# Two fused transformer layers on one core: one input sequence loaded in 32x32 squares and transposed by VectorE, and a set of TensorE transposes moved behind the last quantized down tile

## Chip, cores and metric

One core of a Trainium2 chip runs the whole program. The metric is the device time of that core in microseconds, the median of several runs. Times inside the profile count from the start of its span.

## What is computed

Two layers are applied to x of 2 sequences by 512 rows by 512 features, each layer an attention and a feed-forward part, each part followed by a residual sum and a layer norm:

```
x = layernorm(x + L0_attn(x))     x = layernorm(x + L0_ffn(x))
x = layernorm(x + L1_attn(x))     x = layernorm(x + L1_ffn(x))

L0_attn:  q   = elu(x @ Wq.T + bq) + 1             # only head 0 of each group of 4 is used: 8 heads of 128
          num = q @ M[h] ;  den = q @ z[h] + 1e-6
          out = repeat(num / den, 4) @ Wo.T        # so the four Wo blocks of a group can be summed first
L0_ffn:   ternary weights; silu(gate) * up and the down product are each scaled, clipped and truncated to int8
L1_attn:  q, k, v = x @ Wqkv + b ;  softmax(q k / sqrt(128)) v @ Wo + bo      # one head of 128
L1_ffn:   (silu(x @ Wg.T) * (x @ Wu.T)) @ Wd.T
```

The memory M and z of the first attention are only read; their update is not part of the result.

## The kernel before

The kernel is one long program in Tile. Engines work their own instruction queues strictly in order. A scheduler arranges the instructions of TensorE, VectorE, ScalarE and SyncE from the order of the program text and its own estimates when the kernel is built; GpSimd keeps the order of the text (`manual_schedule`, L59). `tc.issue_after` ties an instruction to stand behind another one. SyncE issues nearly all DMAs. They use eight completion semaphores in turn, so a DMA waits on its queue until the eighth DMA before it has landed, and whatever stands behind it waits too.

**First attention, set-up (L284 to L469).** Rows of x arrive in tiles of 128 rows (`load_x`, L74). A product needs x with the features on the partitions, so each sequence is turned: `transposed` (L106) makes 16 TensorE transposes of 128x128 (L115) into PSUM and copies them (L119), odd k on VectorE and even k on ScalarE, into a tile `xt` of 128 x 4 x 512. `queries` (L328) makes one head of one sequence: four matmuls over k (L334), exp and relu on ScalarE (L340, L342), and their combination on VectorE (L344). Sequence 0 comes first, heads 0 to 7, then sequence 1.

Between the queries the weights are prepared. Each head's Wo arrives as two tiles of 128x1024 (L306), from the pool `wop`, which has six buffers, thus three heads' worth (`pair_tile`, L276). `sum_weights` (L355) adds the two tiles (L358), which frees one of them, and adds the halves of the result (L360), which frees the other. GpSimd does this for heads 0, 3, 5 and 7, VectorE for 1, 2, 4 and 6. `fold` (L363) multiplies M[h] with the summed Wo (matmul pmw, L365) and ScalarE writes the result into `mw` (L368); GpSimd has put z into the last column of mw before (L326). With mw, `read` (L370) needs one matmul per head and row tile (L379).

SyncE's queue in this part holds, in order: two row tiles of x, the eight query weights with bq and z, the four row tiles of sequence 1, m, the Wo tiles of heads 0 to 5, the first gate-and-up tile of the quantized feed-forward part (gu0_0, L242, placed at h == 6, L302), the Wo tiles of heads 6 and 7, the other ten gate-and-up tiles, and small weights.

The scale of the ternary gate-and-up weights is the largest value of gu0_0: `largest` (L182, VectorE) takes it per partition, `over_partitions` (L189) turns it on TensorE (pmx_up), and `scales` (L200) spreads it (pbc_up). These two small TensorE instructions stand among the queries of sequence 1, behind query 1 and query 2. After that each gate-and-up tile is divided by the scale on ScalarE and compared on VectorE (`check_up`, L417).

**End of the quantized feed-forward part (L608 to L679).** There are eight down tiles, one for each sequence and 128 rows. For tile i, `down` (L590) makes the matmuls pd, `scaled` (L610) writes the scaled result (ScalarE) and cuts it (VectorE), `added` (L616) truncates on ScalarE (`truncated_parts`, L168), adds the row tile of x on VectorE (L621, L622) and takes the norm's statistics, and `layernorm_apply` (L152) normalises. `f0_down(i)` (L625) runs these steps staggered: down and scaled of tile i, added of i-1, the norm of i-2. The 16 transposes of sequence 0 for the second attention (`xt_a1`, L677) stand in the text before the last down tile; in the built program the first four of them come before its matmuls and twelve behind. The products of q and k (pqk, L778) follow.

```
        for i in range(2, len(order) - 1):
            f0_down(i)
        xt_a1 = [transposed(xs[0], "a10")]
        for i in range(len(order) - 1, len(order) + 2):
            f0_down(i)
```

Of the kernel before, what the change touches and what calls it, by code (L numbers as in the profile page):

```python
# [10 lines left out]
F32 = mybir.dt.float32  # L11
# [3 lines left out]
AF = mybir.ActivationFunctionType  # L15
ALU = mybir.AluOpType
# [3 lines left out]
P = 128  # L20
B, S, HID = 2, 512, 512
NT = S // P
NK = HID // P
NH, G, D = 8, 4, 128
# [3 lines left out]
LN_EPS = 1e-5  # L28
DEN_EPS = 1e-6
LAST = HID - 1  # L30
LENT = 3
TOP12 = -4096
BELOW_HALF = 0.5 - 2.0**-13
# [3 lines left out]
def kernel(  # L37
# [19 lines left out]
    nc = tc.nc  # L57
# [14 lines left out]
    xs = [[], []]  # L72

    def load_x(b):  # L74
        for t in range(NT):
            x = xp.tile([P, HID], F32, tag="x", name=f"x_{b}_{t}")
            eng = nc.scalar if b == 0 and t % 2 else nc.sync
            eng.dma_start(x, x_in[b, ts(t, P), :])
            xs[b].append(x)
# [2 lines left out]
    bq = const.tile([D, NH], F32, tag="bq", name="bq")  # L82
    z = const.tile([D, NH], F32, tag="z", name="z")

    ident = const.tile([P, P], F32, tag="ident", name="ident")
    make_identity(nc, ident)
    ln_eps = const.tile([P, 1], F32, tag="ln_eps", name="ln_eps")
# [4 lines left out]
    nc.vector.memset(den_eps, DEN_EPS)  # L92
    below_half = const.tile([P, 1], F32, tag="below_half", name="below_half")
    nc.vector.memset(below_half, -BELOW_HALF)
    ones = const.tile([P, P], F32, tag="ones", name="ones")
    nc.vector.memset(ones, 1.0)


    rise = psum("rise")
# [4 lines left out]
    copies = []  # L104
# [47 lines left out]
    def layernorm_apply(out, row, stats):  # L152
        mv, rstd = stats
        nc.vector.tensor_scalar(
            out, row, mv[:, 0:1], rstd, ALU.subtract, ALU.mult
        )
# [5 lines left out]
    def truncated_parts(pool, y, n, name):  # L162

        a = pool.tile([P, S], I8, tag="tr_a", name=f"ta_{name}")  # L168
        b = pool.tile([P, S], I16, tag="tr_b", name=f"tb_{name}")
        nc.scalar.activation(a[:n], y, AF.Relu, bias=below_half[:n])  # L170
        nc.scalar.activation(b[:n], y, AF.Relu, bias=below_half[:n], scale=-1.0)  # L171
        return a, b
# [111 lines left out]
    with tc.tile_pool(name="a0w", bufs=1) as a0w, tc.tile_pool(name="a0", bufs=2) as a0:  # L284
        wq = []
        for h in range(NH):
# [5 lines left out]
            if h == 0:  # L292
                nc.sync.dma_start(bq, bq_in)
                nc.sync.dma_start(z, z_in)
        load_x(1)
        m = a0w.tile([D, NH, D], F32, tag="m", name="m")
        nc.sync.dma_start(m, m_in)

        wos = []
        for h in range(NH):  # L300
            halves = []
            if h == 6:  # L302
                gus = up_weights(gu0_in, "0", range(1))
            for j in range(2):
                w = pair_tile(f"wo{h}_{j}")
                nc.sync.dma_start(w, wo0_in[h, :, ts(j, G // 2), :])  # L306
                halves.append(w)
            wos.append(halves)

        gus += up_weights(gu0_in, "0", range(1, len(CHUNKS)))  # L310
        wqkv = const.tile([P, NK, 3 * D], F32, tag="wqkv", name="wqkv")
# [10 lines left out]

        mw = a0w.tile([D, NH, HID], F32, tag="mw", name="mw")
        nc.gpsimd.tensor_copy(mw[:, :, LAST], z)  # L326

        def queries(b, xt, h, cuts=1):  # L328

# [33 lines left out]
        def fold(h):  # L363
            p = psum(f"pmw_{h}")
            nc.tensor.matmul(p, m[:, h, :], wos[h], start=True, stop=True)  # L365
            c = small.tile([P, 1], F32, tag="col", name=f"col_{h}")
            nc.scalar.mul(c, p[:, LAST:], -1.0)
            nc.scalar.activation(mw[:, h, :LAST], p[:, :LAST], AF.Identity, bias=c)  # L368

        def read(b, t, between):  # L370

            x = xs[b][t]
            ys, steps = [], []
            for h0 in range(0, NH, 4):
                four = []
                den = small.tile([P, 4], F32, tag="den", name=f"den_{b}_{t}_{h0}")
                for j in range(4):
                    po = psum(f"po0_{b}_{t}_{h0 + j}")
                    nc.tensor.matmul(  # L379
                        po, qs[b][h0 + j][:, ts(t, P)], mw[:, h0 + j, :],  # L380
                        start=True, stop=True,
                    )
                    nc.scalar.activation(
                        den[:, j : j + 1], po[:, LAST:], AF.Identity, bias=den_eps
                    )
                    four.append(po)
                nc.vector.reciprocal(den, den)
                for j in range(4):
                    d = den[:, j : j + 1]
                    if h0 + j < LENT:  # L390
                        y = a0.tile([P, HID], F32, tag="y", name=f"y_{b}_{t}_{j}", bufs=3)
                        nc.scalar.activation(  # L392
                            y[:, :LAST], four[j][:, :LAST], AF.Copy, scale=d
                        )
                        if ys:
                            nc.gpsimd.tensor_add(  # L396
                                ys[0][:, :LAST], ys[0][:, :LAST], y[:, :LAST]
                            )
                        ys.append(y)
                    else:  # L400
                        steps.append(nc.vector.scalar_tensor_tensor(  # L401
                            x[:, :LAST], four[j][:, :LAST], d, x[:, :LAST], ALU.mult, ALU.add
                        ))
            between(steps)
            nc.gpsimd.tensor_add(x[:, :LAST], x[:, :LAST], ys[0][:, :LAST])
            return steps
# [25 lines left out]
        for h in range(NH):  # L432
            queries(0, xt, h, 1 if h else 2)
            if h == 4:
                sum_weights(nc.gpsimd, 0)
                turn_memory()
                sum_weights(nc.vector, 1)
            elif h == 6:
                xt1 = transposed(xs[1], "a01")
                sum_weights(nc.vector, 2)  # L440
        sum_weights(nc.gpsimd, 3)
        for h in range(NH):
# [81 lines left out]
    with tc.tile_pool(name="f0", bufs=2) as f0:  # L524
# [85 lines left out]
        def scaled(i):  # L610
            y = f0.tile([P, HID], F32, tag="y", name=f"yd_{i}")
            moved[i] = nc.scalar.activation(y, pds[i], AF.Copy, scale=down_scale)
            cut_to_12(y)
            ys[i] = y

        def added(i):  # L616
            b, t = order[i]
            ta, tb = truncated_parts(f0, ys[i], P, f"d{i}")

            x = xs[b][t]  # L620
            nc.vector.scalar_tensor_tensor(x, tb, 128.0, x, ALU.min, ALU.subtract)  # L621
            nc.vector.scalar_tensor_tensor(x, x, -1.0, ta, ALU.mult, ALU.add)  # L622
            stats[i] = layernorm_stats(x, f"f0_{i}")

        def f0_down(i):  # L625
            if i < len(order):
                pds[i] = down(*order[i])
                scaled(i)
            if 0 <= i - 1 < len(order):
                added(i - 1)  # L630
            if 0 <= i - 2 < len(order):

                b, t = order[i - 2]
                with tc.issue_after(taken[f"f0_{min(i, len(order)) - 1}"].ins):
                    layernorm_apply(xs[b][t], xs[b][t], stats[i - 2])

        to_divide[2:2] = [None, None]
        for c in range(3):
# [35 lines left out]
        up(1, 10, moved.values())  # L674
        for i in range(2, len(order) - 1):
            f0_down(i)
        xt_a1 = [transposed(xs[0], "a10")]  # L677
        for i in range(len(order) - 1, len(order) + 2):
            f0_down(i)  # L679

    gus = up_weights(gu1_in, "1", range(6, len(CHUNKS)))
# [487 lines left out]
```

## Time and profile before

| | |
|---|---|
| median of three runs | 481.75 us (481.19, 481.75, 482.28) |
| the profiled execution | 481.89 us |
| its span, from the first to the last instruction | 479.7 us |
| TensorE (PE) busy | 470.9 us, 98% of the span |
| VectorE (DVE) busy | 349.9 us, 73% |
| ScalarE (ACT) busy | 272.5 us, 57% |
| GpSimd (POOL) busy | 115.1 us, 24% |
| TensorE transposes (L115) that the change touches | 16 of sequence 1 from 32.14 us; 16 of sequence 0 from 233.47 us (4) and 236.47 us (12) |
| load of a 512 KB gate-and-up tile | 7.9 us to landing (median of 20) |

How to read it: the page divides the span into 40 slices and gives each engine's busy share of each slice in tenths. A group line names the program line, engine and operation, then the result and its operands, the shapes, how often, the busy time, the mean of one in ns, and the idle time just before with what ended it. A timeline line begins with its start in us and its duration; several alike in a row are merged, with their number behind an x. In the list of waits the columns are who waited, for whom, and then us in total, how many times, and the longest. PEld is TensorE's loading of the stationary operand, SPq is SyncE's queue. A row of a table by windows gives the window, its length, each engine's busy time with its instructions, and then the granted TensorE clock, the busy share of the DMA engines and GB/s. A float32 matmul appears as two records.

### The profile page before, as it was taken

The page shows a single profiled execution, that of the slowest core. Times are in us where ns is not written, and L with a number is a line of the kernel's source. Part 1 is how long each engine was busy: PE and PEld are TensorE (multiplying, and loading weights), DVE is VectorE, ACT ScalarE, POOL GpSimd, SP SyncE. Part 2 cuts the span into 40 slices and gives each one's busy share as a digit, 9 for nine tenths or more (in the row PEclk, how much of TensorE's full clock was granted, in tenths as well). Part 3 has the DMA queues.
Part 4 walks back from the last instruction along what each step waited for, and adds up shares of the span by engine and source line. Part 5 has one row for each costly group of instructions (what it writes and reads, how often), then busy time and mean ns, then how long its engine had stood idle before and what let it go on. Part 6 is the DMA issues. An engine that isn't in the chain of part 4 may idle for free.

```text
span 479.7 us, 5815 instructions
## 1 busy us (share of the span) xinstructions
PE 470.9 (98%) x1891; PEld 329.6 (69%) x1891; DVE 349.9 (73%) x689; ACT 272.5 (57%) x512; POOL 115.1 (24%) x146
## 2 busy tenths in 40 slices
PE   9999999999999999999999999999999999999995
PEld 8454444434487788787766567888788888888885
DVE  1345677677666586756979989997875778999852
ACT  3344899556666867546645834686753565434221
POOL 0344102666530392000464032000000000023211
PEclk9999999999999999999999999999999999999998
DMA  8999700000043001121390000000000000001011
GB/s 303 389 357 336 296 2 0 0 0 1 2 128 110 3 1 26 65 91 34 113 385 2 0 1 1 1 1 0 1 0 1 1 1 1 0 23 40 27 45 44
DMA packets 13748, 33.98 MB, mean 71 GB/s; under 512 B 1872, under 2 KB 2768, under 8 KB 13712
## 3 DMA queue, kind: packets, MB, share of 16 engines
q1 hardware_dynamic: 13280, 32.85, 19.0%
q10 hardware_dynamic: 432, 0.66, 0.4%
q8 instruction: 22, 0.36, 0.3%
q14 instruction: 14, 0.11, 0.1%
HBM read 31.40 MB, written 2.10 MB: 70 GB/s over the span
## 4 chain that ended last, share of the span: by engine, by line
PE 71%; ACT 7%; DVE 5%; issue 3%; POOL 1%; POOLq 0%; DVEq 0%; ACTq 0%
PE pm L977 17%; PE pg_f L539 9%; PE pc L977 9%; PE pu_f L539 9%; PE pdm L1052 7%; PE pd_f L595 4%; PE pdc L1052 4%; DVE x L401 4%; PE pqk L778 3%; PE po L379 2%; ACT y L392 2%; ACT t L411 2%; PE pv L791 1%; PE po L880 1%; PE pot L863 1%
## 5 line engine op out<-in xcount | busy, mean ns | idle before, releaser
L379 PE MATMUL po<-mw,q 128*128 128x512 f32 x128 | 57.1, 598 | 0.4 <-DVE mv_a L142 0.2
L334 PE MATMUL pq<-xt_a,wq 128*128 128x512 f32 (+1 forms) x136 | 56.4, 567 | 0.0
L148 POOL TENSOR_TENSOR rstd_f<-mv_f,ln_eps 128x1 f32<-128x1 f32 x15 | 4.7, 313 | 185.8 <-DVE mv_f L1063 132.1
L379 PEld LDWEIGHTS po<-mw,q 128*128 128x128 f32 x128 | 23.0, 189 | 32.2 <-issue 17.7
L334 PEld LDWEIGHTS pq<-xt_a,wq 128*128 128x128 f32 x136 | 25.5, 190 | 27.5 <-issue 25.5
L977 PE MATMUL pm<-r,it_early 128*128 128x512 f32 x144 | 37.8, 393 | 0.4 <-ACT r L718 0.4
L977 PE MATMUL pm<-r,ugu 128*128 128x512 f32 (+1 forms) x144 | 36.8, 393 | 0.0
L977 PEld LDWEIGHTS pm<-r,it_early 128*128 128x128 f32 x144 | 27.0, 188 | 6.7 <-ACT r L718 0.7
L401 DVE SCALAR_TENSOR_TENSOR x<-po,den,x 128x511 f32<-128x511 f32 x40 | 29.8, 745 | 1.9
L977 PEld LDWEIGHTS pm<-r,ugu 128*128 128x128 f32 (+1 forms) x144 | 26.8, 186 | 6.3
L170 ACT ACTIVATE ta_f<-y_f,below_half 128x512 int8<-128x512 f32 (+1 forms) x22 | 15.9, 722 | 24.4 <-DVE y_f L160 23.9
L988 DVE SCALAR_TENSOR_TENSOR ev_q<-pm,ev_q 128x512 f32<-128x512 f32 (+1 forms) x28 | 19.2, 687 | 14.0 <-PE pm L977 14.0
L396 POOL TENSOR_TENSOR y<-y,y 128x511 f32<-128x511 f32 x16 | 20.3, 1270 | 31.5 <-ACT y L392 30.8
L565 DVE SCALAR_TENSOR_TENSOR it_f<-tb_f,ta_f 128x512 fp32r<-128x512 int16 (+1 forms) x22 | 15.2, 690 | 16.0 <-ACT tb_f L171 15.9
L977 PE MATMUL pc<-r,ugu 128*128 128x512 f32 (+1 forms) x96 | 26.1, 394 | 0.0
L340 ACT ACTIVATE e<-pq,bq 128x512 f32<-128x512 f32 x16 | 11.1, 693 | 25.8 <-PE pq L334 25.8
L413 POOL TENSOR_SCALAR td<-wd,inv_down 128x512 fp32r<-128x512 f32 (+1 forms) x11 | 19.5, 1792 | 24.8 <-DVE inv_down L204 24.4
L539 PE MATMUL pg_f<-xh,tu 128*128 128x512 f32 (+1 forms) x88 | 25.1, 405 | 0.0
L539 PE MATMUL pu_f<-xh,tu 128*128 128x512 f32 (+1 forms) x88 | 24.0, 394 | 0.0
L539 PE MATMUL pg_f<-xl,tu 128*128 128x512 f32 (+1 forms) x88 | 23.9, 393 | 0.0
L539 PE MATMUL pu_f<-xl,tu 128*128 128x512 f32 (+1 forms) x88 | 23.9, 393 | 0.0
L987 ACT ACTIVATE ev_q<-pc 128x512 f32<-128x512 f32 (+1 forms) x28 | 16.4, 591 | 12.1 <-PE pc L977 12.1
(292 smaller groups left out, 1106.0 us busy)
## 6 DMA issues: line engine op xcount, KB each, us to landing
gu<-in_gu SPq DMA_DIRECT2D x20, 512.0 KB, 7.9
wo<-in_wo SPq DMA_DIRECT2D x16, 512.0 KB, 7.6
wd<-in_wd SPq DMA_DIRECT2D x20, 256.0 KB, 4.7
wq<-in_wq SPq DMA_DIRECT2D x8, 256.0 KB, 4.5
out<-x SPq DMA_DIRECT2D x7, 256.0 KB, 2.0
x<-in_x SPq DMA_DIRECT2D x6, 256.0 KB, 5.4
gu<-in_gu SPq DMA_DIRECT2D x2, 384.0 KB, 6.5
wqkv<-in_wqkv SPq DMA_DIRECT2D x1, 768.0 KB, 10.8
```

What stands on the lines that cost most here:

```text
L170: nc.scalar.activation(a[:n], y, AF.Relu, bias=below_half[:n])
L334: nc.tensor.matmul(pq[:, at], wq[h][:, k, :], xt[:, k, at], start=(k == 0), stop=(k == NK - 1),)
L379: nc.tensor.matmul(po, qs[b][h0 + j][:, ts(t, P)], mw[:, h0 + j, :], start=True, stop=True,)
L396: nc.gpsimd.tensor_add(ys[0][:, :LAST], ys[0][:, :LAST], y[:, :LAST])
L401: steps.append(nc.vector.scalar_tensor_tensor(x[:, :LAST], four[j][:, :LAST], d, x[:, :LAST], ALU.mult, ALU.add))
L413: eng.tensor_scalar(out, w, factor, None, ALU.mult)
L539: nc.tensor.matmul(pp[a][:n], t[:, a, i % NK, :n], x2[b][i], start=(i == 0), stop=(i == 2 * NK - 1),)
L595: nc.tensor.matmul(pd, inter[b][c][:n, ts(t, P)], td[c][:n].bitcast(F32R), start=(c == 0), stop=(c == last),)
L977: nc.tensor.matmul(p[:n], w, x, start=(left[id(p)] == begun[id(p)]), stop=(left[id(p)] == 1))
L987: nc.scalar.activation(ev[:n], pc, AF.Copy, scale=CROSS)
L988: nc.vector.scalar_tensor_tensor(ev[:n], pm, MAIN, ev[:n], ALU.mult, ALU.add)
L1052: nc.tensor.matmul(p[:, :w], got[j // 4][1][kind][:n, j % 4], down_parts[j][kind][:, cols], start=(j == 0 and kind == kinds[0]), stop=(j = ...
```

## The change

Sequence 1 of the first attention is no longer turned by TensorE. It is read from memory a second time, in 32x32 squares: 16 DMAs, one for each feature block of 32, bring 32 partitions x 16 x 32 values each, in runs of 32 values (128 bytes). They are placed so that square f of feature block (k, a) lies where its transpose belongs, and four VectorE transposes of 128x512 (one for each k), each of which turns every 32x32 square in itself, yield `xt1`. The squares' tile uses the buffer that mw takes later, so mw is begun only after the last of these transposes (`begin_fold`). The 16 DMAs stand on SyncE's queue in fours behind the Wo tiles of heads 0 and 1. The rows of sequence 1 as such, which the residual sum needs, are loaded behind all Wo tiles.

The second edit lies at the end of the quantized part. The matmuls of the last down tile and its scaling come first, then the 16 transposes, then the truncation of the tile before, tied behind the two ScalarE copies of the transposes. The fourth row tile of each sequence is normalised as soon as the next tile's sum is made (its own, for the last tile), not after the next tile's statistics. The third edit: VectorE sets the constant of ones, which the first matmuls use, first of all.

```diff
@@ -28,6 +28,7 @@
 LN_EPS = 1e-5
 DEN_EPS = 1e-6
 LAST = HID - 1
+SQ = 32
 LENT = 3
 TOP12 = -4096
 BELOW_HALF = 0.5 - 2.0**-13
@@ -82,6 +83,8 @@
     bq = const.tile([D, NH], F32, tag="bq", name="bq")
     z = const.tile([D, NH], F32, tag="z", name="z")
 
+    ones = const.tile([P, P], F32, tag="ones", name="ones")
+    nc.vector.memset(ones, 1.0)
     ident = const.tile([P, P], F32, tag="ident", name="ident")
     make_identity(nc, ident)
     ln_eps = const.tile([P, 1], F32, tag="ln_eps", name="ln_eps")
@@ -92,8 +95,6 @@
     nc.vector.memset(den_eps, DEN_EPS)
     below_half = const.tile([P, 1], F32, tag="below_half", name="below_half")
     nc.vector.memset(below_half, -BELOW_HALF)
-    ones = const.tile([P, P], F32, tag="ones", name="ones")
-    nc.vector.memset(ones, 1.0)
 
 
     rise = psum("rise")
@@ -292,9 +293,13 @@
             if h == 0:
                 nc.sync.dma_start(bq, bq_in)
                 nc.sync.dma_start(z, z_in)
-        load_x(1)
         m = a0w.tile([D, NH, D], F32, tag="m", name="m")
         nc.sync.dma_start(m, m_in)
+
+
+        x_squares = a0w.tile([P, NK, S], F32, tag="mw", name="x_squares")
+        squares = x_in[1].rearrange("(f i) (k a j) -> k a i f j", i=SQ, k=NK, j=SQ)
+        to_load = [(k, a) for k in range(NK) for a in range(P // SQ)]
 
         wos = []
         for h in range(NH):
@@ -305,7 +310,14 @@
                 w = pair_tile(f"wo{h}_{j}")
                 nc.sync.dma_start(w, wo0_in[h, :, ts(j, G // 2), :])
                 halves.append(w)
+                for k, a in to_load[:4]:
+                    nc.sync.dma_start(
+                        x_squares[ts(a, SQ), k].rearrange("i (f j) -> i f j", j=SQ),
+                        squares[k, a],
+                    )
+                del to_load[:4]
             wos.append(halves)
+        load_x(1)
 
         gus += up_weights(gu0_in, "0", range(1, len(CHUNKS)))
         wqkv = const.tile([P, NK, 3 * D], F32, tag="wqkv", name="wqkv")
@@ -322,8 +334,13 @@
 
 
 
-        mw = a0w.tile([D, NH, HID], F32, tag="mw", name="mw")
-        nc.gpsimd.tensor_copy(mw[:, :, LAST], z)
+
+        mws = []
+
+        def begin_fold():
+            mw = a0w.tile([D, NH, HID], F32, tag="mw", name="mw")
+            nc.gpsimd.tensor_copy(mw[:, :, LAST], z)
+            mws.append(mw)
 
         def queries(b, xt, h, cuts=1):
 
@@ -365,7 +382,7 @@
             nc.tensor.matmul(p, m[:, h, :], wos[h], start=True, stop=True)
             c = small.tile([P, 1], F32, tag="col", name=f"col_{h}")
             nc.scalar.mul(c, p[:, LAST:], -1.0)
-            nc.scalar.activation(mw[:, h, :LAST], p[:, :LAST], AF.Identity, bias=c)
+            nc.scalar.activation(mws[0][:, h, :LAST], p[:, :LAST], AF.Identity, bias=c)
 
         def read(b, t, between):
 
@@ -377,7 +394,7 @@
                 for j in range(4):
                     po = psum(f"po0_{b}_{t}_{h0 + j}")
                     nc.tensor.matmul(
-                        po, qs[b][h0 + j][:, ts(t, P)], mw[:, h0 + j, :],
+                        po, qs[b][h0 + j][:, ts(t, P)], mws[0][:, h0 + j, :],
                         start=True, stop=True,
                     )
                     nc.scalar.activation(
@@ -436,7 +453,10 @@
                 turn_memory()
                 sum_weights(nc.vector, 1)
             elif h == 6:
-                xt1 = transposed(xs[1], "a01")
+                xt1 = xtp.tile([P, NK, S], F32, tag="xt", name="xt_a01")
+                for k in range(NK):
+                    nc.vector.transpose(xt1[:, k, :], x_squares[:, k, :])
+                begin_fold()
                 sum_weights(nc.vector, 2)
         sum_weights(nc.gpsimd, 3)
         for h in range(NH):
@@ -613,13 +633,16 @@
             cut_to_12(y)
             ys[i] = y
 
-        def added(i):
+        def added(i, behind=()):
             b, t = order[i]
-            ta, tb = truncated_parts(f0, ys[i], P, f"d{i}")
+            with ExitStack() as tied:
+                for step in behind:
+                    tied.enter_context(tc.issue_after(step.ins))
+                ta, tb = truncated_parts(f0, ys[i], P, f"d{i}")
 
             x = xs[b][t]
             nc.vector.scalar_tensor_tensor(x, tb, 128.0, x, ALU.min, ALU.subtract)
-            nc.vector.scalar_tensor_tensor(x, x, -1.0, ta, ALU.mult, ALU.add)
+            taken[i] = nc.vector.scalar_tensor_tensor(x, x, -1.0, ta, ALU.mult, ALU.add)
             stats[i] = layernorm_stats(x, f"f0_{i}")
 
         def f0_down(i):
@@ -629,10 +652,15 @@
             if 0 <= i - 1 < len(order):
                 added(i - 1)
             if 0 <= i - 2 < len(order):
-
-                b, t = order[i - 2]
-                with tc.issue_after(taken[f"f0_{min(i, len(order)) - 1}"].ins):
-                    layernorm_apply(xs[b][t], xs[b][t], stats[i - 2])
+                normed(i - 2)
+
+        def normed(i):
+
+            b, t = order[i]
+            n = min(i + 1, len(order) - 1)
+
+            with tc.issue_after(taken[n if t == NT - 1 else f"f0_{n}"].ins):
+                layernorm_apply(xs[b][t], xs[b][t], stats[i])
 
         to_divide[2:2] = [None, None]
         for c in range(3):
@@ -674,8 +702,13 @@
         up(1, 10, moved.values())
         for i in range(2, len(order) - 1):
             f0_down(i)
+        i = len(order) - 1
+        pds[i] = down(*order[i])
+        scaled(i)
         xt_a1 = [transposed(xs[0], "a10")]
-        for i in range(len(order) - 1, len(order) + 2):
+        added(i - 1, (copies[-4], copies[-2]))
+        normed(i - 2)
+        for i in range(len(order), len(order) + 2):
             f0_down(i)
 
     gus = up_weights(gu1_in, "1", range(6, len(CHUNKS)))

```

## The prediction

> **What bounds the kernel now.** I read the page's busy table first: TensorE is busy 470.9 of 479.7 us, and its row of tenths has no hole. Its waits come next, since only they and its own work can change the end.
>
> ```profile
> PE   9999999999999999999999999999999999999995
> ...
> PE pqk L778 <- ACT xt_a L119: 1.0, 1, 1.0
> PE pm L977 <- ACT r L718: 0.4, 1, 0.4
> ```
>
> Four waits, 2.8 us in all with the start; the largest that the change touches is 1.0 us ahead of the q and k products of the second attention. So a change wins by taking work off TensorE or closing that wait, and loses where it opens a hole. The rest was read from the timeline around the two places, engine by engine. First TensorE:
>
> ```profile
> 1.15 3.78 PE L101 MATMUL rise<-ones 128*128 128x128 f32 x16 [1.15 <-DVE ones L96]
> ...
> 32.14 1.91 PE L115 MATMUL pt_a<-ident,x 128*128 128x128 f32 x16
> 33.89 7.03 PE L334 MATMUL pq<-xt_a,wq 128*128 128x512 f32 x16
> 40.76 1.88 PE L365 MATMUL pmw<-wos,m 128*128 128x512 f32 x4
> 42.47 3.60 PE L334 MATMUL pq<-xt_a,wq 128*128 128x512 f32 x8
> 45.91 0.27 PE L189 MATMUL pmx_up<-ident,mx_up 128*2 128x128 f32 x1
> ```
>
> The reader is to see that the 16 transposes occupy 33.89 - 32.14 = 1.75 us of a full TensorE, and that pmx_up, the transpose of the maxima of the first gate-and-up tile (over_partitions, L189), stands right behind query 1 of sequence 1. What feeds it, on VectorE and SyncE's queue:
>
> ```profile
> 24.30 1.21 DVE L358 TENSOR_TENSOR wo<-wo,wo 128x1024 f32<-128x1024 f32 x1
> 25.43 0.68 DVE L344 SCALAR_TENSOR_TENSOR q<-e,r 128x512 f32<-128x512 f32 x1
> 26.04 0.68 DVE L360 TENSOR_TENSOR wos<-wo 128x512 f32<-128x512 f32 x1
> ...
> 35.96 1.28 DVE L182 TENSOR_REDUCE mx_up<-gu 128x1 f32<-128x512 f32 x2 [3.31 <-DMA gu<-in_gu]
> ```
> ```profile
> 27.12 0.72 SPq L242 DMA_DIRECT2D gu<-in_gu  x1
> ```
>
> The chain here: VectorE's sum of head 2's two weight tiles (24.30 to 26.72) frees two of the six wop buffers; only then does SyncE issue head 5's two loads, and behind them, in the same queue, gu0_0 at 27.12. It lands at 35.93, the maxima are done at 37.24, and TensorE needs them at 45.91: 8.7 us in hand.
>
> **What the Trainium skill says.** "TensorE: Matmul & The Clock Gate", The HAM clock gate: after a whole window of about 3.4 us without work the array falls to half clock, and it needs a whole busy window to return. The trace agrees at both ends. TensorE's last product ends at 473.9, and the granted clock is 0.50 in 477.3 to 479.6:
>
> ```profile
> 473.80:477.20 3.40, 0.11 (x1) 0.00 (x0) 1.96 (x6) 0.51 (x1) 0.74 (x1) 1.00 0.00 0
> 477.30:479.60 2.30, 0.00 (x0) 0.00 (x0) 0.00 (x0) 0.00 (x0) 0.00 (x0) 0.50 0.32 114
> ```
>
> At the start the 16 rise records take (4.73 - 1.15)/16 = 0.224 us each, and the 16 transposes behind them 2.48 us in place of 1.75. "DMA: Bandwidth & Descriptors", Why small descriptors are slow: a fixed overhead per packet makes 128-byte pieces dearer per byte; the trace has 9 ns for its 32-byte packets, 27 ns for 512 bytes, 159 ns for 4 KB. "VectorE: DVE Perf Modes", The three transpose paths: VectorE turns only 32x32 blocks, 311 ns for 128x128 bf16; no transpose on VectorE is in this trace.
>
> **The change, part by part.** The order of the built program's instructions on each engine (known without a run) decides what follows.
>
> (a) *16 transposes leave TensorE*: -1.75 us. Their four copies (0.68 each on VectorE, about 0.6 on ScalarE) go too.
>
> (b) *Four VectorE transposes T0 to T3 come*: bounded by 0.31 us (the skill, a quarter of the size) and twice the 0.68 us copy of the same 128x512; I take 0.7, scaling the skill's by its per-element part. They lie off TensorE's path; what matters is where they stand (d).
>
> (c) *16 loads of 32x16 pieces of 128 bytes*: 32 pieces per DMA engine and load. Between 9 and 27 ns a piece, by size about 12.6: 0.40 us a load, 6.5 us in all, in place of four loads of 0.65 us (2.6). SyncE issues them at about 0.45 us each, no slower than they drain. Weights behind them come some 4 us later: m and head 0's and 1's tiles are five times 1.28 us (512 KB at the 407 GB/s of 13 to 23 us), so from the last query weight's 10.75 the last square lands at 10.75 + 6.4 + 6.5 + 0.8 = 24.5. At 27 ns a piece it is 32. T3 is needed by TensorE at 40.7, so either is hidden; above 43 ns a piece it isn't.
>
> (d) *VectorE's queue is reordered*, the step that decides. Before: query product q1, sum of head 1, q2, sum of head 2. In the built program the sum of head 1 stands behind q6, T3 behind q7, the sum of head 2 behind q(1,0) (the product of sequence 1, query 0), the sum of head 4 behind q(1,1), and the maxima mx_up behind that. Each engine works its queue in order. TensorE's order has changed too: query (1,0) k=0..2, folds 0 and 1, (1,1) k=0, (1,0) k=3, (1,1) k=1..3, pmx_up. Step by step:
> - Query 7 starts at 32.14 and ends at 35.57 (8 records of 0.429).
> - Three blocks (2.58), two folds (1.72), two blocks (1.72): query (1,0) ends at 41.59. Folds need head 1's sum, q6 at 34.3 + 1.21 + 0.68 = 36.2: in time.
> - Exp and relu: 1.46 us as from 40.76 to 42.22; 43.05. q(1,0) 0.69, first sum of head 2 1.21: 44.96; second sum: 45.65.
> - SyncE, blocked on these, issues head 5's tiles at 45.0 and 45.7 and gu0_0 at 46.05, not 27.12.
> - The DMA queue has by then run empty. Lone 512 KB gu loads (189 to 221 us) land 3.0 to 3.7 us after issue, their first engine after some 3.0: first tile 48.0, gu0_0 two times 1.28 later, 50.6; its last engine, as in later trains, 0.6 to 0.9 behind: 51.4.
> - Maxima 1.28: pmx_up starts at 52.75.
>
> TensorE has ended query (1,1) at 44.17, so it stands for 8.6 us, and pmx_up starts 52.75 - 45.91 = **+6.8 us**. The 1.75 us of (a) are already in this: the wait swallows them.
>
> (e) *The clock falls.* 8.6 us hold at least one whole idle window; the return costs half of 3.4 to 6.8 us of work, 1.7 to 3.4. The start of this trace needed some 5 us (about 7 slow transposes and 9 fast ones explain 2.48 us): **+2.5 us**.
>
> (f) *Moved with it.* GpSimd's copy of z into mw now waits for T3 (38.5); behind it head 3's sum runs at 38.7 to 42.3 rather than 26.9 to 30.9. Head 6's loads wait for that, but SyncE reaches them only at 46.4: nothing. ScalarE's first mw write also waits for T3, done before fold 0. The x rows of sequence 1 move behind head 7's weights; their first reader (read, batch 1) comes tens of us later: nothing. gu0_1 lands at about 60.5 (heads 6 and 7 and four x rows after 50.6); ScalarE wants it at 54.03 + 6.8 = 60.9 or, with (e), later; the next tiles come every 1.28 us and are wanted about every 2.4 or slower: nothing, but without (e) it is close. Ones first: rise up to 0.15 us earlier, swallowed by the wait as well.
>
> (g) *Transposes behind the last down tile.* Now k=0's four stand before pd(7), and ScalarE's copy comes behind four truncations, so pqk waits 1.04 us. After, pd(7) starts at 233.5 and ends at 236.1, 16 transposes end at 238.1; ScalarE has yd(7), then at once the k=0 copy (237.05 to 237.65) and k=2; k=1 (VectorE) is done at 238.8, wanted at 240. The truncations pushed back end about 1 us sooner than now, the last row of sequence 1 is normalised at about 248.5, and its transposes start at 248.7: **-1.0 us** (bounds 0 and -1.04).
>
> Sum: 6.8 + 2.5 - 1.0 = +8.3 us. The profiled execution took 481.89 us (span 479.7, 2.2 around it), 0.14 above the median 481.75: 490.2 for such a run, **490.1 us** against the median.
>
> **Rivals.**
> *1. The clock stays up, or returns at once* (the gate sees 8.6 us otherwise): 481.75 + 6.8 - 1.0 = 487.6. The clock at the end of the trace speaks against it. 12%.
> *2. The squares come slowly*, so T3 is the late one: at 60 ns a piece the last lands at 48.7, T3 ends near 49.4, the chain of (d) moves by some 8.7: about 499. For: strided 128-byte reads are not in the trace. Against: 9 and 27 ns packets around that size. 10%.
> *3. Faster: gu0_0 is there in time.* If it lands by 42.8, TensorE never stops and the two gains stand: 481.75 - 1.75 - 1.0 = 479.0. Price and place: the 6.8 us at pmx_up; the point is issue of gu0_0 by about 38. For: the DMA engines are idle from about 30, and the buffers could be free. Against: the sum that frees them is queued behind q(1,0), which can't exist before 43. 4%. Between, within 0.2%: 2%.
> That VectorE's transposes don't replace TensorE's is excluded: the built program has four for 16.
>
> **Numbers.** Main case 72%: stall +-0.8, clock 1.7 to 3.4, (g) 0 to -1: 488 to 492. Rival 1 reaches down to 487; rival 2 is left out above; high end 493.5 for a late slow engine. Faster 5%, same 2%, slower 93%; within 0.2% (1 us) is about what the measurement of this kernel can't tell from no change.
>
> **What would show it.** TensorE idle some 8 to 9 us before pmx_up, released by VectorE's mx_up, which waited for gu; gu0_0 issued near 46; the granted clock 0.5 for some us after; T0 to T3 early and unwaited; no wait at pqk. Wrong if pmx_up starts before 46, or if query (1,0) waits for T3.

## The result

The changed kernel takes 490.87 us (median; 489.04 to 491.71) against 482.28 us for the kernel before on the same chip (481.19 to 482.48): ratio 1.0179, 95% interval 1.0158 to 1.0199, so 8.6 us slower. 490.1 us was forecast, with 487.0 to 493.5 as the range.

The profiled execution of the changed kernel took 489.04 us, the shortest of its runs, with a span of 487.3 us; the profiled one before had 481.89 and 479.7. The comparison below is of these two, span against span: 7.6 us.

### The profile page after: what moved, and what is told of

Same layout as the page of the kernel before. It is cut to its first block, busy times and chain, and to the rows that moved or that the text cites. A ratio compares the mean times of both kernels' runs of the same rounds, so it can differ in the third digit from the quotient of the medians.

```text
span 487.3 us, 5822 instructions
## 1 busy us (share of the span) xinstructions
PE 469.7 (96%) x1875; PEld 327.6 (67%) x1875; DVE 353.2 (72%) x691; ACT 271.7 (56%) x510; POOL 114.5 (23%) x146
## 4 chain that ended last, share of the span: by engine, by line
PE 70%; ACT 7%; DVE 5%; issue 3%; POOL 1%; POOLq 0%; DVEq 0%; ACTq 0%
PE pm L1010 17%; PE pg_f L559 8%; PE pc L1010 8%; PE pu_f L559 8%; PE pdm L1085 7%; PE pd_f L615 4%; PE pdc L1085 4%; DVE x L418 3%; PE pqk L811 3%; PE po L396 2%; ACT y L409 2%; ACT t L428 2%; PE pv L824 1%; PE po L913 1%; PE pot L896 1%
## 5 line engine op out<-in xcount | busy, mean ns | idle before, releaser
L351 PE MATMUL pq<-xt_a,wq 128*128 128x512 f32 (+1 forms) x136 | 57.7, 578 | 0.0
L361 DVE SCALAR_TENSOR_TENSOR q<-e,r 128x512 f32<-128x512 f32 x16 | 14.1, 882 | 26.1 <-ACT r L359 26.0
```

Of the source, the lines that this page charges most:

```text
L351: nc.tensor.matmul(pq[:, at], wq[h][:, k, :], xt[:, k, at], start=(k == 0), stop=(k == NK - 1),)
```

## The profile after

The page first: TensorE's busy tenths, the granted clock, and the DMA engines' busy share, in slices of 12.2 us.

```profile
span 487.3 us, 5822 instructions
...
PE   9995699999999999999999999999999999999995
...
PEclk9999799999999999999999999999999999999999
DMA  8964991000006000222093000000000000000011
```

One hole, in the fourth and fifth slices (37 to 61 us), with the clock down in the fifth, where the row before had nines throughout. In the fourth slice the DMA engines are at half or less although much is still to be loaded: SyncE has not issued it yet. TensorE's waits (columns: who waited, for whom, us in total, times, longest) name the place:

```profile
PE pmx_up L190 <- DVE mx_up L183: 9.4, 1, 9.4
...
PE pqk L811 <- ACT xt_a L120: 0.3, 1, 0.3
```

The first line is new; the wait of pqk has shrunk from 1.0 to 0.3 us. What VectorE did ahead of mx_up, from its timeline:

```profile
36.85 0.71 DVE L458 STREAM_TRANSPOSE xt_a<-x_squares 128x512 f32<-128x512 f32 x1
42.25 0.69 DVE L361 SCALAR_TENSOR_TENSOR q<-e,r 128x512 f32<-128x512 f32 x1 [4.70 <-ACT r L359]
42.86 1.22 DVE L375 TENSOR_TENSOR wo<-wo,wo 128x1024 f32<-128x1024 f32 x1
44.11 0.69 DVE L377 TENSOR_TENSOR wos<-wo 128x512 f32<-128x512 f32 x1
...
51.44 1.28 DVE L183 TENSOR_REDUCE mx_up<-gu 128x1 f32<-128x512 f32 x2 [3.99 <-DMA gu<-in_gu]
```

The reader is to see the 4.70 us in brackets: VectorE is idle, waiting for ScalarE's relu of query (1,0), and head 2's sum (42.86) stands behind that product. Before, it started at 24.30 us. Not all of this is the order: with the squares' loads between the Wo tiles, the second tile of head 2 landed at 32.39 us instead of 23.35. But from 32.39 on both tiles were there, and only the sum's place in VectorE's queue kept it back. SyncE's queue shows the consequence:

```profile
23.20 21.95 SPq L311 DMA_DIRECT2D wo<-in_wo  x8
45.20 0.42 SPq L243 DMA_DIRECT2D gu<-in_gu  x1
```

Eight Wo loads take 21.95 us to issue, since the last two need head 2's buffers: the first of these two goes out at 44.10, as the first addition ends (42.86 + 1.22 = 44.08). gu0_0 goes out at 45.20 instead of 27.12 and has landed at 51.41. TensorE's timeline then, and the granted clock in windows (the third figure from the right in a row):

```profile
39.03 4.46 PE L351 MATMUL pq<-xt_a,wq 128*128 128x512 f32 x10
52.86 0.37 PE L190 MATMUL pmx_up<-ident,mx_up 128*2 128x128 f32 x1 [9.37 <-DVE mx_up L183]
53.03 4.95 PE L351 MATMUL pq<-xt_a,wq 128*128 128x512 f32 x8
57.90 0.38 PE L201 MATMUL pbc_up<-dg_up,ones 2*128 2x2 f32 x2
```
```profile
48.00:49.00 1.00, 0.00 (x0) 0.00 (x0) 0.00 (x0) 0.00 (x0) 0.00 (x0) 0.96 0.97 365
49.00:55.00 6.00, 2.14 (x4) 1.14 (x5) 1.85 (x4) 0.00 (x0) 3.60 (x2) 0.50 0.99 371
55.00:56.00 1.00, 1.00 (x2) 0.33 (x2) 0.98 (x1) 0.00 (x0) 0.00 (x0) 0.63 1.00 397
```

A mean of 0.96 in the first window puts the fall at 48.92, and 0.63 in the last puts the return at 55.74. From pmx_up to pbc_up it is 5.04 us; before it was 3.64 (45.91 to 49.55) for the same work.

The sum in spans: pmx_up starts 52.86 - 45.91 = 6.95 us later; the slow clock adds 5.04 - 3.64 = 1.40; pqk starts at 246.53 instead of 239.17, so 8.35 - 7.36 = 0.99 is won back between pbc_up and pqk, where the second edit lies. That makes 7.36; the span grew by 7.6, and the last 0.2 arises behind pqk, from a cause that is not known.

## The experiments

The theory: VectorE's new order delays the sum of head 2, this delays gu0_0's load, pmx_up waits for it, and the clock falls during the wait. The rivals: the squares' small transfers or VectorE's transposes cost the time; the clock has no part in it; the second edit does nothing or harm. "Before" is the kernel before on the same chip, 481.7 to 482.0 us in all these sets.

**The second edit alone**, put into the kernel before (its diff, cut):

```diff
+        i = len(order) - 1
+        pds[i] = down(*order[i])
+        scaled(i)
         xt_a1 = [transposed(xs[0], "a10")]
-        for i in range(len(order) - 1, len(order) + 2):
+        added(i - 1, (copies[-4], copies[-2]))
+        normed(i - 2)
+        for i in range(len(order), len(order) + 2):
             f0_down(i)
```

> The kernel before with the second edit alone: the transposes into xt_a1 stand behind the last quantized down tile, and the first attention is untouched. Theory: the wait of pqk of 1.04 us at 239 us shrinks to about 0.35 us and the interval from there to the end is otherwise unchanged, so about 1.0 us goes: 481.3 us against 482.3 (ratio 0.998), and the stage ahead of 60 us is as before. Rival, the second edit moves nothing because the end is set elsewhere: 482.3 us (ratio 1.000). Rival, the second edit itself costs: above 482.8 us.

480.99 us against 481.95, ratio 0.9980 (0.9974 to 0.9987). The wait of pqk is 0.3 us. The second edit gains 0.96 us, as the theory had it.

**The first edit alone**: the changed kernel with those lines as they were before.

> The changed kernel with the second edit taken back, so that only the squares and what follows from them are left. Theory: the wait of pmx_up of about 9.4 us stays and the gain of 1.0 us goes: 491.9 us against 482.3 before (ratio 1.020). Rival, the second edit is worth nothing: 490.9 us. Rival, the second edit carries the loss: about 481.

492.64 us, ratio 1.0214 (1.0199 to 1.0229). The whole loss is the first edit's, and without the second it is larger. In this trace pmx_up waits 11.0 us (for the changed kernel 9.4) and the stretch to pbc_up takes 6.55 us, so more than the 1.0 us separates these two profiles.

**VectorE's order**, put into the kernel before: no squares, no VectorE transposes, no second edit.

```diff
-            queries(0, xt, h, 1 if h else 2)
+            step = queries(0, xt, h, 1 if h else 2)
...
-                sum_weights(nc.vector, 1)
             elif h == 6:
...
-                sum_weights(nc.vector, 2)
+                with tc.issue_after(step.ins):
+                    sum_weights(nc.vector, 1)
...
-            queries(1, xt1, h)
+            step = queries(1, xt1, h)
             if h == 0:
-                sum_weights(nc.vector, 4)
+                with tc.issue_after(step.ins):
+                    sum_weights(nc.vector, 2)
...
             elif h == 1:
+                with tc.issue_after(step.ins):
+                    sum_weights(nc.vector, 4)
+                    mx_up = largest(
```

> The kernel before, its loads and TensorE's 16 transposes untouched, with only VectorE's queue put in the order of the changed kernel: the sum of head 1 tied behind the query step of (0,6), that of head 2 behind (1,0), that of head 4 and mx_up behind (1,1). No squares, no VectorE transposes, no second edit. Theory (the order alone makes the loss): head 5's tiles and with them gu0_0 are issued at 45 to 47 us instead of 27, mx_up at 51.5 to 53, pmx_up waits 7 to 9 us, and the clock falls behind it: 491.9 us (490 to 493.5). Rival (the squares, as transfers of 128 bytes or as VectorE's work, make it): 482.3 us.

491.18 us, ratio 1.0192 (1.0167 to 1.0217), 0.7 us from the forecast. TensorE's timeline, SyncE's queue and VectorE's timeline in this kernel:

```profile
42.04 3.60 PE L334 MATMUL pq<-xt_a,wq 128*128 128x512 f32 x8
53.34 0.37 PE L189 MATMUL pmx_up<-ident,mx_up 128*2 128x128 f32 x1 [7.70 <-DVE mx_up L182]
```
```profile
22.60 0.90 SPq L242 DMA_DIRECT2D gu<-in_gu  x2
```
```profile
46.97 2.32 DVE L347 SCALAR_TENSOR_TENSOR q<-e,r 128x512 f32<-128x512 f32 x1 [2.60 <-ACT r L342]
49.22 2.28 DVE L362 TENSOR_TENSOR wo<-wo,wo 128x1024 f32<-128x1024 f32 x1
51.41 0.67 DVE L182 TENSOR_REDUCE mx_up<-gu 128x1 f32<-128x512 f32 x1
```

A hole of the same kind in the same place, with none of the squares in the program, but not by the chain of the theory. The ties on VectorE moved SyncE's queue too: gu0_0 went out at 22.60 us, ahead of the Wo tiles of head 4, landed at 29.04, and mx_up did not wait for it. What is late here is mx_up's own place, behind the query step of (1,1) and head 4's first addition. These two took 2.32 and 2.28 us, beside GpSimd's additions from 46.40 to 50.41 us; in the changed kernel they took 0.69 and 1.22. So the run shows that VectorE's order can cost as much without the squares; that a late load does, it does not show, and that the time came out as forecast is luck. The run with the first edit alone lies 1.5 us higher, but their intervals overlap.

**The squares with another order**: the changed kernel whole, with VectorE's queue tied so that the sums of heads 1 and 2 and mx_up come earlier. `queries` gets a parameter `behind`, whose steps its VectorE product is tied to:

```diff
+        hold = ()
         for h in range(NH):
-            queries(0, xt, h, 1 if h else 2)
+            step = queries(0, xt, h, 1 if h else 2, hold)
+            hold = ()
             if h == 4:
+                with tc.issue_after(step.ins):
+                    hold = (sum_weights(nc.vector, 1),)
...
+        with tc.issue_after(step.ins):
+            mx_up = largest(
...
-            queries(1, xt1, h)
+            queries(1, xt1, h, behind=() if h else (taken["up"],))
```

> The changed kernel whole, squares and second edit in it, with VectorE's queue tied: the sum of head 1 behind the query step of (0,4) and ahead of (0,5), that of head 2 between (0,6) and (0,7), mx_up behind the last square transpose and ahead of (1,0). Theory: gu0_0 is issued at about 35 us and lands at 41 to 42, mx_up is done by 43.5, about when TensorE comes to pmx_up (44.2), so the wait is under 0.5 us, the 1.75 us of the transposes and the 1.0 us of the second edit come through: 479.5 us (479 to 481), faster than both. Rival (the squares' small transfers or VectorE's transposes themselves cost): stays near 490, or at least above 484.

481.61 us, ratio 0.9997 (0.9988 to 1.0006): 9.3 us below the changed kernel, so the squares as such do not carry the loss. But the hoped 479.5 did not come. Two waits of TensorE are left, 1.6 us at pmx_up and 1.3 us in `read`. VectorE's timeline and GpSimd's show what made gu0_0 late (it lands at 43.71):

```profile
35.37 2.88 DVE L381 TENSOR_TENSOR wos<-wo 128x512 f32<-128x512 f32 x1
38.17 1.75 DVE L364 SCALAR_TENSOR_TENSOR q<-e,r 128x512 f32<-128x512 f32 x1
```
```profile
35.35 2.34 POOL L379 TENSOR_TENSOR wo<-wo,wo 128x1024 f32<-128x1024 f32 x1
37.77 1.60 POOL L381 TENSOR_TENSOR wos<-wo 128x512 f32<-128x512 f32 x1
```

Head 2's second addition, 0.69 us elsewhere, took 2.88, and the next product 1.75 instead of 0.69: each ends about 0.55 us after GpSimd's addition beside it has ended. The Trainium skill, "SBUF — State Buffer", Who interferes with whom, says that a VectorE instruction with two inputs in SBUF, `tensor_tensor` among them, contends with a GpSimd instruction that reads SBUF, and SBUF: two separate sides, that the shared ports are an exclusive lock held for the whole instruction. The trace fits both, though 0.55 us is a little less than the 0.69 that such an instruction takes alone (GpSimd's spans are rough).

**gu0_0 early**: in the program text the load alone is moved.

```diff
-            if h == 6:
+            if h == 4:
                 gus = up_weights(gu0_in, "0", range(1))
```

> The changed kernel with one edit: the load of gu0_0 stands ahead of head 4's Wo tiles in SyncE's queue instead of behind head 5's. VectorE's queue still has the sums of heads 1 and 2 behind the query steps of (0,6) and (1,0), and mx_up behind (1,1) (the sum of head 4 now stands behind mx_up). Theory: gu0_0 lands at about 35 us, mx_up runs right behind the query step of (1,1) at 45.5 to 46.8, pmx_up starts at about 47.0 instead of 52.9, so some 3.4 us of TensorE's wait stay and the clock falls little or not at all: 484.5 us (483 to 486). If the late load were all of the loss: 479 to 480. If the load's place did not matter: 490.9.

485.91 us, ratio 1.0071 (1.0046 to 1.0096): more than half of the loss is gone. pmx_up starts at 47.15, as expected, 52.86 - 47.15 = 5.7 us earlier; the wait that is left, 3.4 us, comes from mx_up's place behind product (1,1). The 5.7 us are not the load alone, since the built program put head 4's sum behind mx_up as well: in the changed kernel VectorE stood 3.99 us for the load, and the other 1.7 us are about that sum (1.9 us). What was not expected is the clock:

```profile
46.00:47.00 1.00, 0.00 (x0) 0.00 (x0) 1.00 (x2) 0.00 (x0) 0.00 (x0) 0.61 0.95 250
47.00:53.00 6.00, 5.85 (x8) 2.56 (x9) 2.32 (x5) 0.00 (x0) 0.14 (x1) 0.50 0.87 247
53.00:54.00 1.00, 1.00 (x4) 0.29 (x2) 0.00 (x0) 0.20 (x1) 1.00 (x1) 0.98 0.86 279
```

It falls at 46.22, 2.4 us after TensorE's last product (43.79), and returns at 53.04; pmx_up to pbc_up takes 6.55 us, 2.9 more than at full clock. The shorter wait costs more clock than the 9.4 us one. The four runs of this kernel split the same way: three at 485.73 to 486.49 with a mean clock of 0.991 to 0.993, one at 483.30 with 0.997.

**TensorE kept busy in the hole**: 17 matmuls that nobody reads, laid ahead of pmx_up in the changed kernel.

```diff
             elif h == 1:
+                keep = psum("keep")
+                for _ in range(17):
+                    nc.tensor.matmul(keep, ones, xt1[:, 0, :], start=True, stop=True)
                 top_up = over_partitions(mx_up, "up")
```

> The changed kernel with 17 extra multiplications of 128x512 (ones by a block of xt_a, into a PSUM tile that nobody reads; added work, the outputs are those of the changed kernel) between the queries of (1,1) and pmx_up, about 7.5 us of work laid into TensorE's wait of 9.4 us. Theory: the wait for mx_up ends at the same time, 52.9 us, but the clock stays up behind it, so the 1.4 us of the profiled run (more in others, their mean clocks were lower) come back: 489.0 us (488 to 489.6) against 490.9. Rival, the clock costs nothing: 490.9. Rival, the extra work delays pmx_up: above 491.

493.40 us (493.22 to 493.70), ratio 1.0245 (1.0231 to 1.0259). The fill was sized wrongly: a float32 matmul is two records of 0.434 us and I had counted one, so the fill takes 14.76 us and itself delays pmx_up:

```profile
44.14 14.76 PE L475 MATMUL keep<-xt_a,ones 128*128 128x512 f32 x34
58.73 0.27 PE L190 MATMUL pmx_up<-ident,mx_up 128*2 128x128 f32 x1
```

It answers the question all the same. The clock stays at 1.00 and the stretch to pbc_up is 3.64 us again. pmx_up is 58.73 - 52.86 = 5.87 us later than in the changed kernel; less the 1.40 us of slow clock, the span should be 487.3 + 4.47 = 491.8, and it is 491.9. The slow clock is a cost of its own, beside the wait.

**The same with 9 matmuls.**

> As the run with 17 extra multiplications, with 9 of them: in its trace one took 0.87 us (two records of 0.434 us each), so 9 take 7.8 us and end at about 52.0 us, ahead of mx_up. Added work that nobody reads; the outputs are those of the changed kernel. Theory: pmx_up starts at 52.9 us as in the changed kernel, the stretch from pmx_up to pbc_up takes 3.6 us instead of 5.0, and the time is 490.9 less 1.4 to 2.9: 488.0 to 489.5 us. Rival, the clock costs nothing behind the wait: 490.9 us.

490.88 us (488.12 to 491.34), ratio 1.0176 (1.0152 to 1.0200). By its median a miss: in the traced run gu0_0 landed only at 53.9, the fill had ended at 52.3, 3.0 us of wait were left and the clock fell in them. Of its five runs one kept the full clock (mean 0.999) and took 488.12; four had 0.995 and took 490.80 to 491.34. That agrees with the theory, but with one trace I can't say how much of those 2.7 to 3.2 us is clock and how much a later landing.

**A version meant to beat both**: the changed kernel with sums still earlier, and the squares' loads behind head 2's Wo tiles, so that they no longer stand between the first six.

```diff
-                for k, a in to_load[:4]:
...
-                del to_load[:4]
             wos.append(halves)
+            if h == 2:
+                for k, a in to_load:
...
-        load_x(1)
         gus += up_weights(gu0_in, "0", range(1, len(CHUNKS)))
+        load_x(1)
...
+            if h == 2:
+                with tc.issue_after(step.ins):
+                    hold = (sum_weights(nc.vector, 1),)
...
-                begin_fold()
-        sum_weights(nc.gpsimd, 3)
+        with tc.issue_after(sum_weights(nc.gpsimd, 3).ins):
+            begin_fold()
```

> Meant to beat both. The changed kernel, squares and second edit in it, with the squares' loads behind head 2's Wo tiles, the sums of heads 1 and 2 tied behind the query steps of (0,2) and (0,3), mx_up tied between the last square transpose and the query step of (1,0), the copy of z tied behind GpSimd's sum of head 3, and the x tiles of the second sequence loaded behind the up tiles. Theory: gu0_0 lands at about 35 us, pmx_up has no wait at 44.2, gu0_1 lands well ahead of ScalarE's need, and 1.75 + 1.0 us come through: 479.2 us against 482.0 before, and 2.3 less than with the order tied alone. Rival (ScalarE's checks from 50 to 80 us are the bound once TensorE is earlier): 480.3 to 481.0, the same as the second edit alone. Rival (a new load is late): 481 to 484.

480.11 us, ratio 0.9965 (0.9959 to 0.9972): faster than both, 0.9 us short of the theory. pmx_up starts without a wait at 44.30, but TensorE waits 1.2 us in `read` for ScalarE's y. ScalarE is busy without a gap there (8.00 of 8.00 us in 56 to 64 and in 64 to 72), and was in the kernel before: TensorE's gain is kept only if ScalarE's run of comparisons starts earlier too. It did not, since VectorE was held at 49.4 us by GpSimd's sum of head 7 (its additions run from 47.22 to 52.32):

```profile
49.41 1.77 DVE L380 TENSOR_TENSOR wos<-wo 128x512 f32<-128x512 f32 x1 [0.70 <-PE pmw L386]
51.11 1.75 DVE L363 SCALAR_TENSOR_TENSOR q<-e,r 128x512 f32<-128x512 f32 x1
52.79 0.74 DVE L210 SCALAR_TENSOR_TENSOR junk<-t,sc_up,gu 128x512 int8<-128x512 f32 x1
```

**Head 4's sum earlier**, so that head 7's tiles come earlier and GpSimd is done with them before 49 us.

```diff
             elif h == 6:
+                p0 = product(0)
+                with tc.issue_after(step.ins):
+                    hold = (sum_weights(nc.vector, 4),)
...
-                sum_weights(nc.vector, 4)
...
-                fold(0)
+                fold(0, p0)
```

> The kernel with the sums first and the squares behind them (480.1 us), with one more move: head 0's product into PSUM stands behind the query of (0,6), which frees a buffer, and the sum of head 4 is tied behind the query step of (0,6) and ahead of (0,7), so that head 7's tiles are asked for at about 38 us instead of 42.6 and GpSimd's sum of head 7 starts at about 43.5 instead of 47.2. Theory: VectorE's sum of head 6 and query step of (1,2) at 49.4 to 52.8 us took 1.77 and 1.75 us beside GpSimd's sum of head 7; without it they take 0.7 each, the checks of the up tiles start some 1.5 us earlier, TensorE's wait of 1.2 us for ScalarE in the reading stage goes, 479.0 us (478.6 to 479.6). Rival (ScalarE's own work from 50 to 80 us sets that wait): stays at 480.1.

480.07 us, ratio 0.9958 (0.9945 to 0.9972): nothing gained. Its premise did not arise: in this trace head 3's second tile landed at 36.1 us instead of 32.6, all that hangs on it moved, and GpSimd's sum of head 7 ran from 49.58, again beside VectorE's products. That trace is of the slowest of its five runs (481.25 us). It leaves the question open.

**Head 7's sum given to VectorE**, at a place where VectorE has time.

```diff
-                sum_weights(nc.gpsimd, 7)
...
+            elif h == 4:
+                with tc.issue_after(step.ins):
+                    nc.vector.tensor_add(wos[7][0], wos[7][0], wos[7][1])
+                wos[7][1] = None
             elif h == 5:
+                with tc.issue_after(step.ins):
+                    sum_weights(nc.vector, 7)
```

> The kernel with the sums first and the squares behind them (480.1 us), with head 7's sum taken from GpSimd and given to VectorE, its two additions tied behind the query steps of (1,4) and (1,5). Theory (VectorE was held at 49.4 to 52.8 us by GpSimd's sum of head 7, and ScalarE, busy without a gap from 56 to 79 us, could not start its checks earlier): the query step of (1,2) and the sum of head 6 take 0.7 us each, the first check stands at about 50.7 us instead of 52.8, ScalarE's row of y at 76.6 to 77.0 instead of 78.2, TensorE's wait of 1.2 us there goes: 478.9 us (478.5 to 479.5). Rival (two more additions on VectorE hold up ScalarE as much as they save): 480.1. Rival (the sum is late for fold 7): above 481.

478.35 us (478.23 to 478.75), ratio 0.9927 (0.9914 to 0.9941). The same three instructions:

```profile
49.40 0.69 DVE L381 TENSOR_TENSOR wos<-wo 128x512 f32<-128x512 f32 x1 [0.69 <-PE pmw L387]
50.01 0.68 DVE L363 SCALAR_TENSOR_TENSOR q<-e,r 128x512 f32<-128x512 f32 x1
50.61 0.74 DVE L210 SCALAR_TENSOR_TENSOR junk<-t,sc_up,gu 128x512 int8<-128x512 f32 x1
```

The first comparison stands at 50.61 instead of 52.79, ScalarE's row of y at 76.39 instead of 78.18, and TensorE's wait there is gone: every step the theory named. This is the fastest version, 3.4 us under the kernel before and 12.5 under the changed one. It is 0.6 us more than the 1.75 and 1.0 us that were to be won. In the traces the products of `read` account for it (34.71 us from the first one to pf_up, before 35.31); why they ran closer is not known.

## Why the prediction was right

The mechanism of step (d) is what happened: the trace of the changed kernel has every link of it. The runs bear on it from three sides. With the load moved, pmx_up starts 5.7 us earlier; with the squares under another order of the sums and of mx_up, the loss is gone; with work laid into the hole, the clock's part is gone. That the late load alone would do it without the squares is not shown. By its steps:

- **(a), TensorE's transposes**: their 1.75 us are lost in the wait, as said. With the wait gone they were not free to take either: 0.9 us of them came through until VectorE's hold-up was removed as well.
- **(b), VectorE's transposes**: 0.70 to 0.71 us each, 0.7 taken. The prediction does not show how it scaled the skill's figure to this.
- **(c), the squares**: 13.0 ns a piece (8192 packets of 128 bytes), 12.6 taken. The last one landed at 27.4 us instead of 24.5. SyncE needed 2.03 us to issue four of them, and the DMA engines' busy share was 0.99 to 1.00 from 14 to 25 us at only 208 to 234 GB/s; which of the two set the pace is not settled. Hidden from TensorE all the same, as said, but not from head 2's tiles, which stood behind them in the queue (32.39 us instead of 23.35): that step (d) does not count.
- **(d), the order**: head 2's sum at 42.86, the second addition done at 44.80 (45.65 taken); gu0_0 issued at 45.20 (46.05), landed at 51.41 (51.4); pmx_up at 52.86 (52.75). +6.95 us against +6.8. That it is so close is luck in part, for two misses of about 0.85 us cancel. TensorE began its queries at 6.33 instead of 7.21 us, so all that hangs on them came earlier (in the traces of all versions this start lies anywhere from 6.33 to 7.51); and gu0_0 took 6.2 us from issue to landing instead of 5.35. In the traces of the first edit alone and of the nine matmuls, which have the same chain, it landed at 54.2 and 53.9, and pmx_up started at 55.67 and 55.35. The wait itself is 9.37 us instead of 8.6.
- **(e), the clock**: 1.40 us in the profiled run, 2.5 taken, 1.7 the least that was allowed. This is the term that was mis-sized for that run. It counted on a whole window of 3.4 us of work before the clock returns; here the return came 55.74 - 52.86 = 2.88 us after pmx_up had started, and half of that is 1.44. The traces with a wait in the same place gave 1.3, 1.4, 1.6 and, twice, 2.9 us: the clock changed on a grid, and what counts is how much of a slow stretch lies behind pmx_up. The other runs of the changed kernel have mean clocks of 0.983 to 0.989 against 0.992, and take 490.1 to 491.7 us; a larger clock loss would explain them, and so would a later landing of gu0_0 as in the two traces named at (d). These runs have no traces, so the 1.8 us between the profiled run and the median stay unsplit.
- **(f), what moved along**: GpSimd's copy of z at 37.62 and its sum of head 3 behind it, gu0_1 landing at 61.4 us with ScalarE taking it at 62.9: nothing lost, as said. With the ones set first, rise started 0.11 us earlier. In the repaired versions what moved along was not nothing: with the wait gone, GpSimd's sums met VectorE's work.
- **(g), the second edit**: 0.99 us in the traces, 0.96 by itself, 1.0 taken. But "no wait at pqk" was wrong: 0.35 us are left. I had let ScalarE copy block k=0 as soon as four transposes were done. The built program goes by row tiles, so that block k=0 is complete with the 13th of 16; ScalarE's copies start at 245.89, 1.6 us after the first transpose.

The sum for the profiled run was 490.2 us, and it took 489.04. Of the 1.2 us, 1.1 is the clock (e); and 1.7 us of this run lie outside its span, where the prediction carried over the 2.2 of the run before. The 0.2 us behind pqk and the 0.1 of (d) go the other way. The median, 490.87, is 0.8 above the forecast 490.1; since the profiled run was the shortest, how its terms look in a median run is not known.

Of the rivals, that the clock stays up and that the squares are slow are refuted by these traces. The one that ended faster (gu0_0 in time, 479.0) named the right point: once the load was issued at 30 us (480.1) and VectorE was free as well (478.4), the gains stood.

## What to carry to other kernels

A change that removes work from a full engine and gives it to another can also rewrite queues, so read the built order: here, with four transposes of 0.7 us added to VectorE's queue, a sum of 1.9 us came to stand behind a product, and the load of gu0_0, which waited for that sum, went out 18 us later. Read the built order of the other engines too: in the run that only tied VectorE's instructions, the same load moved on SyncE's queue. Follow each buffer from the instruction that frees it to the transfer that takes it, and ask what stands behind that transfer in the same queue. Then add the clock as a cost of its own for a hole of some 3 us or more (3.0 us lowered it here, 1.6 us did not), with a range (1.3 to 2.9 us here) and not a value.

## What was not expected of the hardware

- **The clock's slow stretches came in whole steps, and the steps need not be wholly idle or busy.** They lasted 6.82 us (48.92 to 55.74) in the changed kernel, 6.82 (46.22 to 53.04) with gu0_0 early, and 13.66 (47.92 to 61.58) with the first edit alone: two, two and four times 3.41. The two other slow stretches, of VectorE's order in the kernel before (49.70 to 56.54) and of the nine matmuls (54.66 to 58.08), are two steps and one. The Trainium skill, "TensorE: Matmul & The Clock Gate", What's actually happening, gives a free-running window of 3413 ns and says that the clock falls after at least one idle window of about 3.4 us and rises after at least one busy one. The grid agrees. The thresholds don't quite. The steps with gu0_0 early, the first figure behind the length being TensorE's busy time (ends of matmuls are modelled):

```profile
42.80:46.21 3.41, 0.99 (x3) 0.16 (x1) 3.35 (x5) 1.27 (x2) 0.00 (x0) 1.00 0.17 53
46.21:49.63 3.42, 2.48 (x4) 1.21 (x5) 2.65 (x6) 0.00 (x0) 0.00 (x0) 0.50 0.83 242
49.63:53.04 3.41, 3.41 (x5) 1.35 (x4) 0.46 (x1) 0.00 (x0) 0.18 (x1) 0.50 0.94 250
```

  A step with 0.99 us of work was followed by the fall, and one with 2.48 us was not yet followed by the return. In the other traces the fall followed steps with 0.00, 0.00, 0.12 and 1.05 us of work, and did not follow one with 1.40 us (42.09 to 45.50 in the changed kernel); the return followed steps with 2.72, 2.88, 3.20 and 3.42 us, and not one with 2.49. So the same hole can cost more or less, by where it lies in the steps.
- **GpSimd's additions hold VectorE's.** VectorE's 0.69 us additions and products took 1.75 to 2.88 us beside a GpSimd addition in the lines above, while its transposes did not: one ran from 35.53 to 36.23 in the version meant to beat both, beside GpSimd's addition from 35.14 to 36.74, in 0.70 us.
